# One planner for every expert block of a mixture-of-experts layer

## The chip, the cores and the metric

One NeuronCore of a Trainium2 chip runs the whole program. The metric is device time in microseconds (us) of one execution; a median of runs is given, and one further execution was recorded by the hardware profiler. The engines are TensorE (PE, matmuls), VectorE (DVE), ScalarE (ACT), GpSimd (POOL) and SyncE (SP, which here only issues DMAs). Each engine works through its own instructions strictly in order; semaphores tie the engines together.

## The reference

There are 16 sequences of 256 tokens with 256 features, 4096 tokens in all. `x` goes through an adapter with a layer norm; every token is then given to two of eight experts, and all tokens also go through one shared expert:

```python
y = adapter_layernorm(x, profile_id)               # per sequence
p = softmax(y @ gate_w + gate_b); v, i = top_k(p, 2); v = v / (v.sum() + 1e-9)
mlp(y, w1, b1, w2, b2) = gelu(y @ w1 + b1) @ w2 + b2        # 256 -> 1024 -> 256
out = x + y + mlp_shared(y) + sum_k v_k * mlp_expert[i_k](y)
```

## The kernel before

**Blocks.** Tokens are sorted by expert through DRAM. A *unit* is one block of 256 tokens of one expert (`nt=2`) or of 128 tokens (`nt=1`, a half block). Units 0 to 15 are static: two for each of the eight experts. Units 16 to 36 take what is left: 16 full blocks and five half blocks (`HALF_AT`), whose expert is read from a table at run time. Each number is split into two fp16 parts, so that a product takes three matmuls.

**One unit.** `mm1` (L669) makes eight chunks of the hidden layer, six matmuls each; ACT applies the gelu to each chunk (L676) from one of four PSUM banks into one of two `h` buffers; after four chunks DVE or ACT writes the high half of `hh` (L686 or L684) and DVE the low half (L690); `mm2` (L705) makes the output in eight pieces of six matmuls; DVE takes it out of PSUM (`take`, L1249), and POOL scatters the rows to the DRAM tensor `yrow` with an indirect DMA (`scatter_y`, L1255). A half block has matmuls of 128 columns in `mm1` and four pieces in `mm2`.

**What feeds a unit.** `block_T` (L1242, L1246) brings the transposed tokens and their row numbers, `block_weights` (L1606, L1608) two weight pieces of 1 MB and a small tail, into one of three weight buffers, for a full block only if the expert changed. Both are issued by SP.

**The early sums.** Six of the sixteen sequences (`EARLY = 6`) get their weighted expert sums while the late blocks still run. Such a sum needs a load of the sequence's rows of `yrow` (`y_load`, L1631, 512 KB, on SP) and four DVE operations (`combine`, L1648), after which SP stores the sequence. A load reads `yrow`, so it waits for the scatters that stand ahead of it in the program. In the same stretch SP loads each sequence of `x` again (`x_again`, L1664), and POOL adds it and a bias (`add_x`, L1669 and L1670).

**Order.** Two mechanisms set the order of instructions. Class `Plan` is a list scheduler: each operation has an engine (or a choice of two), a planned duration, things it must wait for (`deps`, after their planned end; `after`, after their planned start), buffers it takes from pools, and a wish time `v`. `schedule` always takes the operation that can start first; `v` decides between equals. In the kernel before, the plan covers everything up to the first half of unit 13. From there to the end of the shared block 13 a loop written by hand follows (L1681 to L1712). It sets the order of SP and POOL; the order on PE, DVE and ACT follows the framework's own scheduling of that recording. In it `unit_steps` alternates chunk c of a unit's `mm1` with piece c of the unit before in `mm2`; at step 7 of unit s the loop stores sequence s-23, sums sequence s-22 and loads sequence s-21:

```python
if n == 7:
    b = s - EARLY_AT - 2
    if 0 <= b < EARLY: store(b)
    b = s - EARLY_AT - 1
    if b in early: combine(b, early.pop(b), lean=True)
    b = s - EARLY_AT
    if 0 <= b < EARLY: early[b] = y_load(early_buf[b % 2], 2 * b, 2)
```

**The end.** All engines then meet at a branch (L1714, L1715) that would do rare extra blocks. After it a second, small plan does the rest of the shared blocks 13 to 15 and the sums of sequences 6 to 15 (L1759 to L1793). There a sequence in `POOLED` (the even ones) has its second addend scaled by ACT (L1773) and added by POOL (L1788); the others take two more DVE operations (L1780).

Of the kernel before, what the change touches and what calls it, by code (L numbers as in the profile page):

```python
# [19 lines left out]
P = 128  # L20
# [4 lines left out]
E = 8  # L25
# [12 lines left out]
EARLY_AT = TOP_AT + 3  # L38
# [13 lines left out]
NPLAN = 14  # L52
# [3 lines left out]
POOLED = tuple(range(0, NB, 2))  # L56
# [95 lines left out]
VE2 = 8.9  # L152


@with_exitstack
def adapter_moe_kernel(
# [559 lines left out]
    def plan_unit(k, v, xin, w, tail, evac, x_deps, w_deps, t_deps, only1=False, xrel=(), free_hi=True):  # L716

        w1 = views(w)[0]
        g1, ge, quads = [], [], []
        for c in range(NC):  # L720
            a = ("u", k, c)
            vc = v + 1.29 * c
            g1.append(
                plan.op(
                    "PE", 0.645, lambda c=c, a=a: mm1(pa_of(a), xin(), w1, c, BLK), vc,
                    [*x_deps, w_deps[0]] + g1[-1:], acq=[("pa", a)], lat=0.25,
                    rel=xrel if c == NC - 1 else (),
# [6 lines left out]
                    "ACT", 0.5,  # L734
                    lambda c=c, a=a, hb=hb: gelu(
                        h32b[plan.slot["h32", hb]], pa_of(a), tail, c, BLK
# [4 lines left out]
            if c % 4 == 3:  # L741
                def hi(act, q=q, hb=hb):
                    split_hi(hhb[plan.slot["hh", k]], h32b[plan.slot["h32", hb]], tail, q, BLK, act)

                def lo(q=q, hb=hb):
                    split_lo(hhb[plan.slot["hh", k]], h32b[plan.slot["h32", hb]], tail, q, BLK)

                h = plan.op(
                    ("DVE", "ACT") if free_hi else "ACT", (0.87, 1.1) if free_hi else 1.1,
# [5 lines left out]
                    plan.op("DVE", 1.28, lo, vc + 2.0, [h], rel=[("h32", hb)], lat=0.05)  # L755
# [3 lines left out]
        plan_g2(k, v + 10.3, w, evac, [quads[0], quads[1]], w_deps[1])  # L759
        return g1  # L760

    def plan_g2(k, v, w, evac, quads, w_dep):
        w2 = views(w)[1]
        g2 = []
        for c in range(2 * 4):
            q, t = place(c, 2)
            r = (f"py{t}", k)
            g2.append(
                plan.op(
                    "PE", 0.645,  # L770
                    lambda q=q, t=t: mm2(py_of(t, k), hhb[plan.slot["hh", k]], w2, q, t),
                    v + 1.29 * c + 0.65, [quads[0 if q < 2 else 1], w_dep] + g2[-1:],
                    acq=[r] if q == 0 else (), rel=[("hh", k)] if c == 7 else (), lat=0.25,
                )
            )
            if q == 3:
                evac(t, g2[-1], v + 1.29 * c + 1.5, (r,))

# [345 lines left out]
    def table(last):  # L1124
# [104 lines left out]
        plan.op("DVE", 1.0, meta, 300.0, [got])  # L1229
        plan.op("DVE", 0.1, lambda: V.memset(spot, 0.0), 0.0, [got, o], add=["pa", "py0", "py1"])  # L1230
        return got, pads
# [21 lines left out]
    def scatter_y(ysb, idt, t):  # L1253
# [9 lines left out]
        apart("ysc", ins)  # L1263

# [59 lines left out]
    def shared(b, only1=False):  # L1324
        def evac(t, mm, v, rel):
# [9 lines left out]
            ("s", b), U0 + b * PU, lambda: xlnT[:, b], halves(wsh), tsh, evac,  # L1335
            [tc_done[b]], pE.done, [pE.tail1], free_hi=False,
        )

    for b in range(NSH):
        shared(b)  # L1340
    got, pads = table([s for sc in scats for s in sc])
# [20 lines left out]
    def static_unit(s):  # L1362
        u = units[s]
        e = s // NSTAT
        vu = U0 + (NSH + s) * PU
        BT[s] = plan.op(
            "SP", 5.2,
            lambda: block_T(u, xgb[plan.slot["xg", s]], idb[plan.slot["id", s]]),
            vu - 22.0, [got, *pads, null_row, *[o for sc in scats for o in sc]],
            acq=[("xg", s), ("id", s)], land=2 * P * 1024,  # L1370
        )

        def evac(t, mm, v, rel):
            ty = plan.op(
                "DVE", 0.45,
                lambda: take(ysbb[plan.slot["ysb", (s, t)]], py_of(t, ("e", s)), u["tail"]),
                v, [mm, prep[e].tail, prep[e].bias], acq=[("ysb", (s, t))], rel=rel,
            )

            def sc():  # L1380
                scatter_y(ysbb[plan.slot["ysb", (s, t)]], idb[plan.slot["id", s]], t)

            plan.op(
                "POOL", 1.36, sc, v + 0.5, [ty],
                rel=[("ysb", (s, t))] + ([("id", s)] if t == 1 else []), land=P * 1024,
# [5 lines left out]
            [BT[s]], prep[e].done, [prep[e].tail], only1=s == NPLAN - 1,  # L1391
            xrel=[("xg", s)],
        )
        g1_last[s] = g1[-1]
# [465 lines left out]
```

## Time and profile before

| what | value |
|---|---|
| median of 3 runs | 651.94 us (650.79 to 653.05) |
| the profiled execution | 656.57 us |
| its span on the core, first to last instruction | 654.8 us |
| PE, busy share of the span | 93% |
| DVE | 63% |
| ACT | 60% |
| POOL | 37% |
| mean granted TensorE clock | 0.959 |
| DMA traffic | 134.71 MB, mean 206 GB/s |

The profile shows one execution. Its page gives busy time by engine, busy tenths in 40 slices of the span (16.4 us each) with the granted TensorE clock, and groups of instructions; further answers of the trace give waits, windows of time and the instructions in order of time.

### The profile page before, as it was taken

What the parts mean: (1) busy time and instruction counts of PE and PEld (TensorE: products, weight loads), DVE (VectorE), ACT (ScalarE), POOL (GpSimd) and SP (SyncE); (2) the same over time, 40 slices, a digit from 0 to 9 for tenths busy, and PEclk for the clock granted to TensorE, in tenths of its full rate; (3) what the DMA queues carried; (4) which work ended last, traced back from release to release, by engine and by line L of the source; (5) the groups of instructions that cost most, each with busy time, mean ns of one, the idle gap of its engine ahead of it and who ended that gap; (6) DMA issues with size and microseconds to landing.
All of it is one profiled execution on the core that took longest, in us unless ns stands there. A gap on an engine that the chain in (4) does not pass through costs nothing. (4 is left out here: it accounts for less than half of the span.)

```text
span 654.8 us, 15253 instructions
## 1 busy us (share of the span) xinstructions
PE 610.2 (93%) x5542; PEld 525.9 (80%) x5542; DVE 414.2 (63%) x992; ACT 390.7 (60%) x609; POOL 241.7 (37%) x367
## 2 busy tenths in 40 slices
PE   4699999999999999999999999999678899999895
PEld 3368887888988888888888888987556789989684
DVE  5678889899863635676658544454347654556377
ACT  1378576796776868879889544444232344444462
POOL 1003466285386013232222122333336455645222
PEclk8579999999999999999999999999797899999899
DMA  7775559847322394978995598288787579990093
GB/s 261 256 273 165 174 189 320 292 188 244 135 95 88 88 276 130 261 247 217 246 301 170 111 363 241 54 202 215 240 262 238 135 228 341 168 282 27 23 376 106
DMA packets 95784, 134.71 MB, mean 206 GB/s; under 512 B 53691, under 2 KB 73173, under 8 KB 87766
## 3 DMA queue, kind: packets, MB, share of 16 engines
q1 hardware_dynamic: 88130, 113.09, 59.0%
q0 software_dynamic: 6768, 18.43, 8.3%
q10 hardware_dynamic: 804, 2.16, 1.0%
q8 instruction: 45, 0.74, 0.4%
q14 instruction: 37, 0.30, 0.2%
HBM read 96.46 MB, written 44.42 MB: 215 GB/s over the span
## 5 line engine op out<-in xcount | busy, mean ns | idle before, releaser
L705 PEld LDWEIGHTS <-hh 128*128 128x128 f16 x2424 | 235.2, 99 | 51.1 <-DVE hh L686 11.9
L705 PE MATMUL bank<-wst,hh 128*128 128x256 f16 x1536 | 213.7, 277 | 14.2 <-DVE hh L686 9.4
L676 ACT ACTIVATE h<-bank,tst 128x256 f32<-128x256 f32 x256 | 139.5, 562 | 129.4 <-PE bank L669 109.2
L669 PE MATMUL bank<-late,wst 128*128 128x256 f16 x1536 | 205.0, 274 | 0.7 <-ACT h L676 0.7
L1255 POOL DMA_INDIRECT yrow<-late,idt x69 | 88.7, 1286 | 265.3 <-DVE late L1249 224.5
L669 PEld LDWEIGHTS <-wst 128*128 128x128 f16 x1536 | 151.0, 98 | 18.8 <-issue 0.9
L669 PE MATMUL bank<-xlnT,wsh 128*128 128x256 f16 x768 | 106.0, 277 | 3.2 <-ACTq L1715 3.2
L705 PE MATMUL bank<-wsh,hh 128*128 128x256 f16 x768 | 102.6, 274 | 3.1 <-DVE hh L690 3.1
L676 ACT ACTIVATE h<-bank,tsh 128x256 f32<-128x256 f32 x128 | 70.1, 561 | 58.0 <-PE bank L669 55.3
L690 DVE SCALAR_TENSOR_TENSOR hh<-h,tst,hh 128x1024 f16<-128x1024 f32 x64 | 85.7, 1339 | 17.1 <-ACT hh L684 16.2
L669 PEld LDWEIGHTS <-wsh 128*128 128x128 f16 x768 | 75.3, 100 | 15.0 <-issue 3.7
L1099 POOL DMA_INDIRECT xslot<-late,sli x64 | 71.6, 1118 | 38.5 <-issue 22.5
L686 DVE TENSOR_SCALAR hh<-h,tst 128x1024 f16<-128x1024 f32 x45 | 39.8, 885 | 72.1 <-ACT h L676 72.0
L1249 DVE SCALAR_TENSOR_TENSOR late<-bank,tst 128x256 f32<-128x256 f32 x64 | 30.6, 478 | 35.6 <-PE bank L705 34.6
L690 DVE SCALAR_TENSOR_TENSOR hh<-h,tsh,hh 128x1024 f16<-128x1024 f32 x32 | 41.0, 1281 | 17.4 <-ACT hh L684 17.2
L676 ACT ACTIVATE h<-bank,late 128x128 f32<-128x128 f32 x40 | 18.3, 458 | 32.7 <-PE bank L669 23.4
L684 ACT ACTIVATE hh<-h,tsh 128x1024 f16<-128x1024 f32 x31 | 35.6, 1147 | 0.8
L1088 POOL IOTA late<- 128x32 int32 x32 | 4.8, 162 | 75.1 <-PE bank L965 39.5
L1648 DVE SCALAR_TENSOR_TENSOR base<-xlnT,wts,base 128x256 f32<-128x256 f32 x24 | 10.4, 479 | 34.2 <-DMA xlnT<-yrow 34.1
L624 DVE SCALAR_TENSOR_TENSOR wst<-wf,prep,wst 128x1024 f16<-128x1024 f32 x20 | 25.3, 1276 | 0.1
L1670 POOL TENSOR_TENSOR base<-base,sb_b 128x512 f32<-128x512 f32 x16 | 23.4, 1462 | 1.3
L830 PE MATMUL bank<-xlnT,wst 128*128 128x256 f32 x64 | 19.7, 436 | 4.1 <-DMA wst<-in_adp_dram 4.1
(233 smaller groups left out, 599.5 us busy)
## 6 DMA issues: line engine op xcount, KB each, us to landing
wst<-scr SPq DMA_DIRECT2D x32, 1024.0 KB
scr<-wst SPq DMA_DIRECT2D x16, 1024.0 KB
wf<-scr SPq DMA_DIRECT2D x10, 1024.0 KB
wf<-in_ew_dram SPq DMA_DIRECT2D x5, 1028.0 KB
wf<-in_ew_dram SPq DMA_DIRECT2D x5, 1024.0 KB
wst<-in_adp_dram SPq DMA_DIRECT2D x16, 256.5 KB
xlnT<-in_xT_dram SPq DMA_DIRECT2D x16, 256.0 KB
base<-in_x_dram SPq DMA_DIRECT2D x16, 256.0 KB
```

The source lines that it names most:

```text
L624: V.scalar_tensor_tensor(self.w[:, a + 2048 : b + 2048], self.wf[h][:, f], sc[:, 2 * h : 2 * h + 1], self.w[:, a:b], ALU.mult, ALU.subtract,)
L669: mm = PE.matmul(pa[:, 0:n_tok], w1[:, wl, c, k, :], xin[:, xl, k, 0:n_tok], start=i == 0, stop=i == len(seq) - 1,)
L676: ACT.activation(h32[:, c % 4, 0:n_tok], pa[:, 0:n_tok], AF.Gelu_apprx_tanh, bias=tail[:, c : c + 1], scale=tail[:, 8:9],)
L684: ACT.activation(hi, h4, AF.Copy, scale=tail[:, 9:10])
L686: V.tensor_scalar(hi, h4, tail[:, 9:10], None, ALU.mult)
L690: V.scalar_tensor_tensor(hh[:, 1, c, 0:n_tok], h32[:, :, 0:n_tok], tail[:, 9:10], hh[:, 0, c, 0:n_tok], ALU.mult, ALU.subtract,)
L705: PE.matmul(py, hh[:, hl, k, t * P : (t + 1) * P], w2[:, wl, k, :], start=q == 0 and i == 0, stop=q == 3 and i == len(seq) - 1,)
L830: PE.matmul(pt_of(("z", b))[:, 0:S], wa()[:, k * P : (k + 1) * P], xf32(b)[:, k, :], start=k == 0, stop=k == KC - 1,)
L1099: ins = POOL.indirect_dma_start(out=xslot[:, :], out_offset=bass.IndirectOffsetOnAxis(ap=sli[:, c, j : j + 1], axis=0), in_=payb[plan.slot ...
L1249: V.scalar_tensor_tensor(ysb, py, tail[:, 10:11], tail[:, 11 : 11 + D], ALU.mult, ALU.add)
L1255: ins = POOL.indirect_dma_start(out=yrow[:, :], out_offset=bass.IndirectOffsetOnAxis(ap=idt[:, t, :].bitcast(I32), axis=0), in_=ysb, in_of ...
L1670: POOL.tensor_tensor(bb, bb, sb2_b.unsqueeze(1).broadcast_to([P, 2, D]), ALU.add)
```

## The change

`plan_unit` and `plan_g2` learn half blocks (`nt=1`) and a looser rule for expert blocks and late shared blocks: a chunk follows the one before it by its planned start, no longer by its planned end. `static_unit` becomes `expert_unit`, which plans all 37 units, with their weight loads (`W`), and with wish times 10.32 us apart, where static ones had 16.4. Reloads of `x`, the additions on POOL, the loads of `yrow`, each single addition of an early sum and the stores become operations of the same plan. The reloads of `x` are issued from ACT's queue instead of SP's. The load of sequence b is planned for unit b+22, its sum for unit b+23, the store for b+24. The hand-written loop with its helpers goes. In the last plan all sequences but 14 and 15 use ACT and POOL for the second addend.

```diff
     def plan_unit(..., nt=2, behind=None):
+        n, step = nt * P, 0.645 * nt
+        full = nt == 2
+        loose = k[0] == "e" or k[1] >= NSH
...
-                    "PE", 0.645, lambda c=c, a=a: mm1(pa_of(a), xin(), w1, c, BLK), vc,
-                    [*x_deps, w_deps[0]] + g1[-1:], acq=[("pa", a)], lat=0.25,
+                    "PE", 0.645 if full else 0.5, lambda c=c, a=a: mm1(pa_of(a), xin(), w1, c, n), vc,
+                    [*x_deps, w_deps[0]] + ([] if loose else g1[-1:]), acq=[("pa", a)], lat=0.25,
+                    rel=xrel if c == NC - 1 else (), after=g1[-1:] if c else [behind],
...
-    def static_unit(s):
+    def expert_unit(s, vu):
         u = units[s]
-        vu = U0 + (NSH + s) * PU
+        nt = u["nt"]
+        last = None if s == 0 else BT[s - 1]
         BT[s] = plan.op(
-            "SP", 5.2,
+            "SP", 2.6 * nt,
             lambda: block_T(u, xgb[plan.slot["xg", s]], idb[plan.slot["id", s]]),
-            vu - 22.0, [got, *pads, null_row, *[o for sc in scats for o in sc]],
+            vu - TV, [got, *pads, null_row, *[o for sc in scats for o in sc]],
+            after=[last] if s >= NS else [], acq=[("xg", s), ("id", s)], land=nt * P * 1024,
+        )
...
+            W[s] = plan.op(
+                "SP", 2.4, lambda: block_weights(u), vu - WV, deps, acq=acq, land=P * (6500 if nt == 2 else 13000)
+            )
...
-            prep[e] = Prep(e, U0 + (NSH + NSTAT * (e - 1)) * PU - 8.0, after=after, split_after=split)
+            prep[e] = Prep(e, v_of(NSTAT * (e - 1)) - VP, after=after, split_after=split)
...
+    for b in range(NB):
+        s = TOP_AT + 1 + b
+        o = plan.op(
+            "ACT", 0.45,
+            lambda b=b, xr=xr: ACT.dma_start(
+                xr, x[b * S : (b + 1) * S, :].rearrange("(t p) d -> p t d", p=P)
+            ), vu_of[s], wf_free, after=[g1_of[s][2]], acq=[("xr", ("xr", b))], land=P * 2048,
+        )
+        x_op = plan.op(
+            "POOL", 2.6, add_x, vu_of[s] + 12, [o], rel=[("xr", ("xr", b))],
+            after=[g1_of[s + 1][2]] if s + 1 < NU else [],
+        )
+        if b < EARLY:
+            s += 3
+            o = plan.op(
+                "SP", 0.45, lambda b=b, yl=yl: y_load(yl, 2 * b, 2), vu_of[s],
+                [*wf_free, sc_last[NS - 1]], after=[g1_of[s][3]], acq=[("ey", ("ey", b))],
+                land=P * 4096,
+            )
+            for i in range(4):
+                o = plan.op(
+                    "DVE", 0.45, lambda b=b, yl=yl, i=i: sum_one(b, yl, i // 2, i % 2, wts),
+                    vu_of[s + 1] + 6, [o, wts_op], after=[g1_of[s + 1][4]] if i == 0 else [],
+                    rel=[("ey", ("ey", b))] if i == 3 else (),
+                )
+            plan.op("SP", 0.45, lambda b=b: store(b), vu_of[s + 2], [o, x_op], after=[g1_of[s + 2][3]])
+
+    shared(NSH, v_end, only1=True)
...
-    with tc.manual_schedule(engines={ET.SP, ET.Pool}):
-        xr = None
-        early = {}
-        for s in range(NPLAN, NU):
-            u = units[s]
-            for n, _ in enumerate(unit_steps(block_unit(u))):
-                if n == 6 and s + 2 < NU:
-                    next_T(units[s + 2])
-                if n == 7:
...
-            if NS <= s + 2 < NU and units[s + 2]["nt"] == 2:
-                block_weights(units[s + 2])
-            if xr is not None:
-                add_x(s - TOP_AT - 2, xr)
-            if TOP_AT < s <= TOP_AT + NB:
-                xr = x_again(s - TOP_AT - 1)
...
-                    if c == 1 and bb in POOLED:
+                    if c == 1 and bb < NB - 2:
                         done.append(plan.op(
                             "ACT", 0.42,
...
-                            "DVE", 0.45,
+                            "DVE", 0.48,
```

## The prediction

> **What bounds the kernel now.** I read the page's slices first. TensorE is nearly always busy, so what counts is where it is not.
>
> ```profile
> PE   4699999999999999999999999999678899999895
> PEclk8579999999999999999999999999797899999899
> ```
>
> Apart from start and end, one hole stands in slices 29 to 32 (458 to 524 us), where the granted clock drops as well. Windows of 20 us sharpen it (columns: window, length, then busy us and instruction count of PE, PE weight loads, DVE, ACT, POOL, then clock, DMA share, GB/s):
>
> ```profile
> 400.00:420.00 20.00, 20.00 (x195) 18.04 (x193) 9.72 (x12) 8.82 (x17) 5.02 (x7) 1.00 0.52 154
> 440.00:460.00 20.00, 18.57 (x182) 16.32 (x180) 8.67 (x11) 8.04 (x15) 6.34 (x6) 1.00 0.81 194
> 460.00:480.00 20.00, 13.13 (x102) 10.37 (x100) 9.37 (x19) 4.28 (x9) 7.50 (x9) 0.83 0.83 256
> 480.00:500.00 20.00, 14.48 (x110) 11.43 (x108) 10.14 (x12) 5.91 (x11) 9.24 (x8) 0.83 0.70 207
> 500.00:520.00 20.00, 17.90 (x179) 15.76 (x177) 13.39 (x20) 7.83 (x15) 9.12 (x10) 0.99 0.81 225
> ```
>
> PE idles 1.43 + 6.87 + 5.52 + 2.10 = 15.9 us in the last four. No engine is full there, so this is a chain of waits. The wait lists, PE's, DVE's and SP's in turn, name its links (total, times, longest):
>
> ```profile
> PE bank L705 <- DVE hh L686: 10.7, 5, 4.5
> PE bank L705 <- DVE hh L690: 8.6, 9, 2.7
> ```
>
> ```profile
> DVE base L1648 <- DMA xlnT<-yrow: 34.1, 6, 7.4
> ```
>
> ```profile
> SPq L1631 <- DMA yrow<-late,idt: 55.2, 7, 29.3
> ```
>
> PE waits for the split of `hh` on DVE, DVE stands six times before an early sum (L1648) until its load of `yrow` has landed, and that load waits on SP for a scatter (the 29.3 is a seventh, at the end). The timeline shows one turn:
>
> ```profile
> 450.58 1.77 POOL L1255 DMA_INDIRECT yrow<-late,idt  x1 [0.34 <-DVE late L1249]
> ...
> 457.63 0.39 SPq L1631 DMA_DIRECT2D xlnT<-yrow  x1
> ...
> 461.33 1.27 DVE L1648 SCALAR_TENSOR_TENSOR base<-xlnT,wts,base 128x256 f32<-128x256 f32 x3 [6.58 <-DMA xlnT<-yrow]
> 463.31 0.74 DVE L686 TENSOR_SCALAR hh<-h,tst 128x1024 f16<-128x1024 f32 x1
> 464.11 0.39 PE L705 MATMUL bank<-wst,hh 128*128 128x256 f16 x2 [3.72 <-DVE hh L686]
> ```
>
> From the scatter's issue to the load's is 7.05 us, from there to the sum 3.70: 10.75 us. DVE is idle for 6.58 of them with the finished gelu behind the sum in its queue. The takes wait behind it too, hence the next scatter is late, hence the next load: the six stalls (6.04, 6.58, 7.39, 7.44, 2.35, 4.30 us) feed each other. Afterwards the clock costs more. Two groups of six matmuls in a cold stretch and two after it, by their starts:
>
> ```profile
> 495.18 1.49 PE L669 MATMUL bank<-late,wst 128*128 128x256 f16 x6
> 496.46 1.49 PE L705 MATMUL bank<-wst,hh 128*128 128x256 f16 x6
> ...
> 499.67 0.82 PE L669 MATMUL bank<-late,wst 128*128 128x256 f16 x6
> 500.32 0.82 PE L705 MATMUL bank<-wst,hh 128*128 128x256 f16 x6
> ```
>
> 1.28 us a group against 0.65. Over the three cold stretches (465.7 to 472.0, 494.35 to 499.0, 519.2 to 523.5) the groups take 2.9 + 2.3 + 1.7 = 6.9 us more than at 0.655. The hole costs 15.9 + 6.9 = **22.8 us**.
>
> **Part 1, the early sums.** In the built order I count the matmuls between the three instructions (0.109 us for 256 columns, half for 128). Before, scatter to sum is 5.9, 6.1, 5.5, 5.2, 5.9 and 6.9 us of matmuls against the 10.75 needed. In the changed kernel it is 13.7, 14.1, 9.3, 19.7, 15.7 and 14.1, since the sum moves one unit behind the load. Five are clear by 3 us or more; the third is short by 1.4 us. Before, a DVE stall of 2.35 us cost PE nothing and one of 4.30 cost 2.1 plus the cold 1.7, so I take 0.5 for it (0 to 2). SP still stands up to 7 us before such a load, with token and weight loads behind it; in the built order these lead their first matmul by 12.8 us or more at nearly every late unit (9.5 at two; least before, 9.0), so that is hidden; without this cover each late us is one of PE's. Gain 22.8, loss 0.5.
>
> **Part 2, blocks 14 to 36 in the plan.** Matmuls, gelus, splits, takes and scatters keep number and shape. From 525 to 600 us PE shows no idle in the old alternation, so there is nothing to win. The plan places `mm2` as soon as its inputs are ready by its own durations. Most are near the trace (gelu 0.58 with latency against 0.56, split 0.87 and 1.28 against 0.753 and 1.283); two are not. Six matmuls of 128 columns are planned at 0.5 us and start 0.33 apart, so PE arrives up to 8 x 0.17 = 1.4 us early at what it needs, in five half blocks: 0 to 7 us. And the plan does not know that POOL's 32 additions slow DVE: a low split of 1.28 us took 2.55 beside one. About 2 us of slack stand against that after the last chunk (four alternations of 1.31 = 5.2 us less the chain 0.56 + 0.75 + 1.28 and waits). I take 1.0, nearer to the old order's nothing.
>
> **Part 3, reloads of `x` on ACT.** Sixteen issues of 0.39 us leave SP (6.2 us, hidden there: SP was not on PE's chain but for part 1) and come to ACT. ACT usually idles 0.74 us before each gelu, which hides an issue. New is that ACT waits in order: for POOL's addition two sequences back (7.3 to 16.7 us of matmuls ahead in the built order), and, through shared DMA semaphores, twice for a 1 MB weight piece issued 5.2 and 5.6 us ahead. Behind a waiting ACT stand gelus, behind them PE, covered by four banks, some 5 us in alternation. With pieces landing in 4 to 8 us (1 and 2 MB at 256 GB/s) ACT stands up to 3 us in two places: 0 to 2 us of PE, I take 0.5.
>
> **Part 4, static blocks.** Wish times closer together bring preparations and loads forward relative to the shared blocks. PE idles 1.2 us from 180 to 440, so the bounds are -1.2 and, with ACT 19 of 20 us busy around 350, some +3; I take +0.5. The branch keeps its 3.2 us of PE idle.
>
> **Part 5, the tail.** From 631.5 to 651.5 us the chain that ended last is DVE. DVE loses six operations, 6 x 0.48 = 2.9 us; ACT gains six copies of 0.50, four of them ahead of the last split in its queue; POOL gains three additions. The answer for the additions' line shows how a DVE operation fares beside POOL (min/median/max ns):
>
> ```profile
> L1780 DVE SCALAR_TENSOR_TENSOR base<-wst,wts,base x18: 471/479/1552, 636.8 to 650.3; 128x256 f32<-128x256 f32 x18
> L1788 POOL TENSOR_TENSOR base<-base,wst x3: 1262/1387/1397, 638.1 to 648.2; 128x512 f32<-128x512 f32 x3
> ```
>
> The 30 operations took 18.1 us instead of 30 x 0.48 = 14.4, 0.74 for each of five additions, so three more cost 2.2 and the tail would gain 0.7. The Trainium skill speaks against that (*SBUF — State Buffer*, "SBUF: two separate sides"): VectorE and GpSimd hold a shared port pair for a whole instruction and the loser blocks fully. At 1.3 us each, three more cost 3.9 and the tail loses 1.0. The longest operation, 1.55 us, lies nearer to the page; with the copies ahead of the split I take +0.5 (-2.9 to +2.5).
>
> **Sum.** -22.8 + 0.5 + 1.0 + 0.5 + 0.5 + 0.5 = -19.8. The profiled span 654.8 becomes 635.0, its execution 656.57 becomes 636.8. That execution lies 4.6 above the median of the runs, so the forecast for the median is 651.94 - 19.8 = **632.1 us**.
>
> **Rivals.**
> *Half a gain.* The loads come later than their place says, since POOL carries scatters and additions in one queue and a scatter must itself wait for an earlier load, so three sums still stall. For: the third sum has no slack. Against: the others have 3 to 9 us. Keeping 10 of the 22.8 gives 642.
> *DVE becomes the bound.* With sums in place DVE does 6.9 us a unit (two high splits 1.5, two low 2.6, two takes 1.0, four sums 1.9) and up to 2.5 beside POOL, 9.4 of PE's 10.5. Against: only six units. If the plan's exact placing costs 0.5 us in each of the 23 late units, 11.5 in all, the result is 643.
> *The stall only moves* to another late link (a weight load, a take), PE keeps its hole: 652. Against: leads as above.
> *Slower.* The reloads hold ACT, one mechanism: POOL's addition or a weight piece late, ACT stopped in the gelus. From about 5 us of hold on, PE pays one for one; with 19.8 gained elsewhere the sixteen reloads decide above 1.2 us each, about 6.4 us of hold every time. At 8 us each it is 632 + 16 x 3 less the 0.5 already in the sum, about 680. Against: POOL was 37% busy, and POOL's additions lead by 7.3 us or more.
>
> **How the numbers follow.** Forecast 0.69, half a gain 0.11, DVE or the exact order 0.10, only moved 0.05, slower 0.05. The forecast's own range is 627 (tail and static blocks at their best) to 638. The range for 8 in 10 is 626 to 643: it takes in the two middle rivals and leaves out the last two and their neighbours. Two kernels under 0.3% (2 us) apart can't be told apart here. Faster by more: 0.69 + 0.11 + 0.10 = 0.90, less 0.01 for a middle rival that goes further; the 0.05 of a stall that only moved splits into 0.03 same and 0.02 slower, so same is 0.04 and slower 0.07.
>
> **What would show it.** Right: no PE wait for L686's successor over 1 us between 440 and 505, clock 1.00 in those windows, the sums' wait for `yrow` down from 34.1 us to under 5, last expert matmul about 20 us earlier. Part 3 wrong: ACT waits on DMA or POOL before a gelu of over 4 us. Part 2 wrong: many PE waits of 0.3 to 1 us on `hh`. Part 5: the stretch from branch to end, 36 us now, over 38. The forecast falls if the third sum starts the old convoy again, or if a weight piece comes late behind a waiting load.

## The result: a smaller gain than forecast

The changed kernel takes 644.58 us (median of four runs, 641.56 to 645.63); the kernel before took 652.50 beside it (650.79 to 654.18). The ratio is 0.987, with a 95% interval of 0.983 to 0.992. Forecast were 632.1 us, in a range of 626 to 643: the sign is right, the size is not. In a later session (e5 below) the ratio was 0.981 (0.973 to 0.989). Every ratio here leaves out runs more than 1.5% above the fastest of the same kernel, which matters only for e3 and e4 below, where four of six runs and ten of 22 fall out.

The profiled executions differ by more than the medians: their spans are 654.8 and 642.1 us. The prediction had found that the profiled execution of before lies 4.6 us above its median; that of the changed kernel (643.85 us) lies 0.7 below its own. So of the 12.7 us between the spans some 5 belong to these two executions.

**A ledger of TensorE's loss.** I count each trace back from its end in matmul work (0.1092 us for 256 columns, half for 128) and set the time against it. What is over is idle time or a low clock. "Late" is the stretch from the point where 170 us of this work are left to the branch (143.8 us of work), "tail" is the rest, from the branch to the end.

```
                      before    changed
start of late stretch  446.6      443.6
loss in it              25.0       13.5
branch reached         615.5      600.9
loss in the tail        13.1       15.0
```

So -3.0 ahead of the stretch, -11.5 in it, +1.9 in the tail: -12.6 us, the difference of the spans but for rounding. Of the 3.0, 1.3 belong to Part 4 (below). The other 1.7 lie still earlier, where three traces of the old plan (this one, e17 and e18) differ among themselves by 2.9. The page's slices of the changed kernel show the same:

```profile
PE   5599999999999999999999999999988998999795
PEclk7779999999999999999999999999999999999798
```

The two slices at 8 and the 8 further on are the old hole, flatter; its clock stays up. The windows of 20 us (columns as in the prediction):

```profile
440.00:460.00 20.00, 20.00 (x209) 18.20 (x207) 10.31 (x15) 12.12 (x22) 4.05 (x6) 1.00 1.06 264
460.00:480.00 20.00, 17.93 (x161) 15.29 (x159) 7.00 (x12) 8.31 (x15) 8.50 (x11) 1.00 0.75 215
480.00:500.00 20.00, 16.47 (x172) 14.54 (x170) 13.95 (x19) 10.06 (x20) 11.51 (x12) 1.00 0.81 249
500.00:520.00 20.00, 19.45 (x179) 17.18 (x178) 13.73 (x18) 9.91 (x17) 12.32 (x14) 1.00 0.65 164
520.00:540.00 20.00, 16.82 (x175) 14.89 (x173) 6.64 (x8) 9.43 (x18) 10.89 (x13) 1.00 1.00 352
```

From 460 to 540 us PE idles 2.1 + 3.5 + 0.6 + 3.2 = 9.4 us, where it idled 14.5 before; the clock, 0.83 in two of these windows before, is 1.00. The lists of waits of PE and of DVE (whole trace: total, times, longest) say on what; of the first line, the longest wait (3.2) lies in the tail and 3.9 us lie ahead of the branch:

```profile
PE bank L704 <- DVE hh L689: 7.3, 8, 3.2
PE bank L668 <- ACT h L675: 6.3, 4, 2.5
```

```profile
DVE base L1534 <- DMA xlnT<-yrow: 9.5, 5, 3.6
```

The sums (L1534, before L1648) wait 9.5 us for `yrow` instead of 34.1, and still five times. PE's second line is all but new (0.7 us, once, before): PE waits for gelus. ACT's list between 440 and 604 us shows why these are late:

```profile
ACT h L675 <- DMA late<-xslot: 8.1, 2, 7.1
ACT h L675 <- DMA out_dram<-base: 6.2, 1, 6.2
ACT h L675 <- POOL base L1562: 5.3, 2, 3.0
```

No gelu needs the store `out_dram<-base`. The reload of `x` in front of it in ACT's queue does: it shares a DMA semaphore with that store, and the other rows are a shared semaphore and POOL's addition.

At first sight the reloads are the culprit. The next view says otherwise. The timeline of the changed kernel, lines of SP, DVE and POOL in order of time:

```profile
446.73 1.03 SPq L1289 DMA_DIRECT2D wst<-scr  x2
447.85 0.39 SPq L1523 DMA_DIRECT2D xlnT<-yrow  x1
...
456.24 1.92 DVE L1534 SCALAR_TENSOR_TENSOR base<-xlnT,wts,base 128x256 f32<-128x256 f32 x4 [1.15 <-DMA xlnT<-yrow]
...
457.25 1.06 SPq L1289 DMA_DIRECT2D wst<-scr  x2
...
459.57 1.00 POOL L1267 DMA_INDIRECT yrow<-late,idt  x1 [12.98 <-DVE hh L689]
...
460.88 0.97 POOL L1267 DMA_INDIRECT yrow<-late,idt  x1 [0.19 <-issue]
...
468.09 0.39 SPq L1523 DMA_DIRECT2D xlnT<-yrow  x1
...
471.86 1.40 DVE L1534 SCALAR_TENSOR_TENSOR base<-xlnT,wts,base 128x256 f32<-128x256 f32 x3 [3.21 <-DMA xlnT<-yrow]
```

From one load of `yrow` (447.85) to the next (468.09) are 20.2 us. The first is issued 1.1 us behind 2 MB of weights in the same queue: by the trace's packets, the weights' 256 of 8 KB run from 447.71 to 454.31 and the load's 256 of 2 KB from 453.32 to 455.65. POOL has nothing to do for 13 us, although the take for its next scatter was done at 449.2: in the program this scatter waits first of all for the load to have landed, since it writes the tensor that the load reads, and that wait ends at 456.17. So scatter, load and next scatter form a loop, each waiting for the one before; a round of it, from load to load, is called a turn below. The scatter after it, issued at 460.88 beside the next 2 MB of weights, has its last packet at 467.36, and the next load waits for that. The sum, at 456.24, stood 1.15 us. It is a reader at the side of this loop, not a link in it.

How far this loop lags I measure as each scatter's start, less the start of the matmul beside which it stands in the built order (start : us late):

```
before   435:0.5 449:7.3 451:5.8 465:10.5 467:9.8 477:7.6 479:6.4 493:10.1 502:2.7 503:1.2 515:5.3 517:4.9 522:0.9
changed  442:0.3 460:10.4 461:9.2 473:12.3 480:14.2 481:15.3 493:12.2 494:12.3 502:11.6 503:10.5 512:7.7 516:8.5 518:9.9 523:3.2 524:1.0
```

In both kernels the lag comes with the first load and goes some 15 us after the sixth. In the changed kernel it is the larger one. The six loads themselves are 3.4, 13.2, 13.0, 10.3, 11.2 and 7.7 us behind their places: the first turn, with weights beside both its load and its scatter, puts the loop 9.8 us back, and four more turns (7.4, 12.2, 8.9 and 9.9 us) win back 5.5.

### The profile page after: what moved, and what is told of

Same layout as the page of the kernel before. It is cut to its first block, busy times and chain, and to the rows that moved or that the text cites. A ratio compares the mean times of both kernels' runs of the same rounds, so it can differ in the third digit from the quotient of the medians.

```text
span 642.1 us, 15142 instructions
## 1 busy us (share of the span) xinstructions
PE 605.6 (94%) x5542; PEld 522.8 (81%) x5542; DVE 405.8 (63%) x969; ACT 404.3 (63%) x632; POOL 234.2 (36%) x370
## 5 line engine op out<-in xcount | busy, mean ns | idle before, releaser
L675 ACT ACTIVATE h<-bank,tst 128x256 f32<-128x256 f32 x256 | 136.0, 560 | 127.8 <-PE bank L668 86.8
L704 PE MATMUL bank<-wst,hh 128*128 128x256 f16 x1536 | 205.8, 273 | 3.3 <-DVE hh L689 3.3
L668 PE MATMUL bank<-late,wst 128*128 128x256 f16 x1536 | 200.4, 273 | 5.0 <-ACT h L675 4.3
L1267 POOL DMA_INDIRECT yrow<-late,idt x69 | 77.6, 1125 | 256.7 <-DVE late L1261 202.6
L704 PE MATMUL bank<-wsh,hh 128*128 128x256 f16 x768 | 104.7, 277 | 3.4 <-DVE hh L689 3.4
L675 ACT ACTIVATE h<-bank,tsh 128x256 f32<-128x256 f32 x128 | 70.1, 560 | 58.7 <-PE bank L668 55.1
L689 DVE SCALAR_TENSOR_TENSOR hh<-h,tst,hh 128x1024 f16<-128x1024 f32 x64 | 89.4, 1396 | 27.5 <-ACT hh L683 26.0
L668 PEld LDWEIGHTS <-wsh 128*128 128x128 f16 x768 | 75.5, 100 | 15.5 <-issue 3.8
L685 DVE TENSOR_SCALAR hh<-h,tst 128x1024 f16<-128x1024 f32 x27 | 21.3, 787 | 46.3 <-ACT h L675 46.3
L689 DVE SCALAR_TENSOR_TENSOR hh<-h,tsh,hh 128x1024 f16<-128x1024 f32 x32 | 42.0, 1311 | 13.4 <-ACT hh L683 13.1
L683 ACT ACTIVATE hh<-h,tst 128x1024 f16<-128x1024 f32 x37 | 42.5, 1148 | 1.1
L683 ACT ACTIVATE hh<-h,tsh 128x1024 f16<-128x1024 f32 x29 | 33.3, 1147 | 0.8
L1100 POOL IOTA late<- 128x32 int32 x32 | 4.8, 161 | 73.4 <-PE bank L977 37.8
L1562 POOL TENSOR_TENSOR base<-base,xlnT 128x512 f32<-128x512 f32 x16 | 20.6, 1285 | 8.2 <-DMA xlnT<-in_x_dram 8.0
```

Of the source, the lines that this page charges most:

```text
L668: mm = PE.matmul(pa[:, 0:n_tok], w1[:, wl, c, k, :], xin[:, xl, k, 0:n_tok], start=i == 0, stop=i == len(seq) - 1,)
L675: ACT.activation(h32[:, c % 4, 0:n_tok], pa[:, 0:n_tok], AF.Gelu_apprx_tanh, bias=tail[:, c : c + 1], scale=tail[:, 8:9],)
L683: ACT.activation(hi, h4, AF.Copy, scale=tail[:, 9:10])
L685: V.tensor_scalar(hi, h4, tail[:, 9:10], None, ALU.mult)
L689: V.scalar_tensor_tensor(hh[:, 1, c, 0:n_tok], h32[:, :, 0:n_tok], tail[:, 9:10], hh[:, 0, c, 0:n_tok], ALU.mult, ALU.subtract,)
L704: PE.matmul(py, hh[:, hl, k, t * P : (t + 1) * P], w2[:, wl, k, :], start=q == 0 and i == 0, stop=q == 3 and i == len(seq) - 1,)
```

## The experiments

Theories: the reloads of `x` hold ACT (1), or the rest of the old convoy costs the time (2; in e1's expectation theory 2 is still the plan's exact order). The second was later split into DVE's sums (A) and the loop of load and scatter alone (B). All results are in one table; medians are of all runs, and "late" and "tail" are TensorE's losses in the one profiled execution, in us. Two traces of the changed kernel itself differ by 1.3 us in the late stretch, so a difference of that size between two rows shows nothing. The expectations quote 24.8 and 13.2 for the late stretches of the two kernels, from a cut that ended 7 us of work ahead of the branch; the table cuts at the branch.

```
                         median  before  ratio (95%)             late  tail
changed, first time      644.58  652.50  0.987 (0.983 to 0.992)  13.5  15.0
e1  reloads on SP        664.29  674.51  0.987 (0.983 to 0.990)  12.1  13.5
e2  old tail             664.48  674.51  0.987 (0.982 to 0.992)  13.0  13.1
e3  both                 663.10  674.51  0.975 (0.968 to 0.983)  13.6  11.7
e4  old, sums later      674.17  674.51  0.995 (0.992 to 0.998)  22.5  13.4
e5  changed, again       640.85  653.92  0.981 (0.973 to 0.989)  12.2  13.9
e6  reloads on POOL      640.88  653.92  0.983 (0.977 to 0.990)  10.9  14.0
e7  no reloads, adds     638.18  653.92  0.979 (0.972 to 0.985)   8.2  15.1
e8  no loads, sums       632.88  653.92  0.971 (0.964 to 0.977)   2.6  15.5
e9  loads, no sums       643.54  654.72  0.983 (0.978 to 0.987)  13.6  14.2
e10 pairs                637.77  654.72  0.975 (0.970 to 0.981)   6.8  15.0
e11 pairs, POOL          636.99  654.72  0.974 (0.969 to 0.979)   3.9  14.3
e12 pairs, POOL, tail    634.35  654.72  0.970 (0.965 to 0.974)   4.0  13.6
e13 loads first          664.59  675.34  0.987 (0.978 to 0.997)  15.4  12.3
e14 loads first, POOL    662.39  675.34  0.983 (0.975 to 0.991)  11.2  15.1
e15 loop alone           658.78  675.34  0.977 (0.969 to 0.984)   7.1  13.9
e16 first, pairs, etc.   662.76  675.34  0.980 (0.972 to 0.988)  10.4  15.5
e17 old, no loads, sums  632.69  653.47  0.967 (0.962 to 0.973)   0.4  14.9
e18 old, pairs           642.74  653.47  0.983 (0.978 to 0.988)  13.2  13.4
```

Runs e1 to e4 and e13 to e16 were on two other chips, where every kernel, the one before included, takes some 20 us more, all of it ahead of the late stretch; so ratios and late losses are compared, not times. e7, e8, e9, e15 and e17 leave out work that the result needs; they show only what a part costs.

**e1, reloads back on SP.**

```diff
-            "ACT", 0.45,
-            lambda b=b, xr=xr: ACT.dma_start(
+            "SP", 0.45,
+            lambda b=b, xr=xr: SP.dma_start(
```

> The changed kernel with one thing undone: the sixteen reloads of x are issued by SP again, in the plan, in place of ACT. Theory 1 (ACT stands in front of its gelus because a reload in its queue waits for a DMA or for POOL's addition): ACT's waits for DMA and POOL before a gelu, 25 us between 440 and 604 us in the changed kernel's trace, are gone, PE's waits for gelus (6.3 us) go and most of those for the low split (3.9 us) with them; time 635 to 639 us, 0.975 to 0.980 of the kernel before. Theory 2 (the plan's exact order, or DVE beside POOL's additions, costs the missing gain): time as the changed kernel, 642 to 646 us, 0.985 to 0.991. Theory 3 (SP needed the relief: its weight loads now come late behind waiting reloads): 650 us or more.

Ratio 0.987, theory 2's number. ACT's waits for DMA and POOL are gone as theory 1 said. But PE still waits 7.6 us for other things (10.9 in the changed kernel), its clock falls to 0.86 in the window from 500 to 520 us, and the late stretch loses 12.1 us. The two largest rows of its waits between 460 and 625 us:

```profile
PE bank L668 <- DMA wst<-scr: 3.5, 2, 1.9
PE bank L704 <- DVE hh L689: 2.8, 2, 2.2
```

With the reloads in SP's queue it is the weights behind them that come late.

**e2 and e3, the old share of the final sums**, alone and with e1.

```diff
-                    if c == 1 and bb < NB - 2:
+                    if c == 1 and bb % 2 == 0:
...
-            if bb < NB - 2:
+            if bb % 2 == 0:
```

> The changed kernel with the final sums shared out as before (ACT copies and POOL additions for every second sequence, not for all but the last two). Theory 1 (the new share costs the tail 1.7 us, 37.84 us from PE's restart behind the branch to the end against 36.15): 642 to 643.5 us, stretch 36 to 36.5 us. Theory 2 (the tail's difference is the clock's, cold for longer behind the branch): stretch stays at 37 to 38 us, time 644 to 645 us.

> Both of the two edits before this one: reloads of x by SP, final sums shared out as before. If both theories 1 hold the gains add up: 633 to 637 us. If neither does: 642 to 646 us.

e2 changes the time by nothing that can be told, and its tail loses 13.1 us against 15.0 and 13.9 of the two traces of the changed kernel. e3's ratio looks better, but it rests on two of six runs, one of them (652.04) 9 us under the other five; the median of all six is 0.983 of the kernel before's. Its late stretch is no better (13.6), its tail is the shortest of all. Over all traces the tail loses 12.3 to 15.5 us with the new share (twelve traces, mean 14.3) and 11.7 to 15.5 with the old (eight, mean 13.6). A difference of 0.7 us within such a spread isn't shown.

**e4, the old kernel with the sums one unit later.**

```diff
-                    b = s - EARLY_AT - 2
+                    b = s - EARLY_AT - 3
...
-                    b = s - EARLY_AT - 1
+                    b = s - EARLY_AT - 2
```

> The kernel before, with nothing but the early sums (and the stores behind them) moved one unit later; blocks 14 to 36 stay outside the plan, reloads of x stay on SP. Theory 1 (the hole between 440 and 525 us is the sums' place alone): the sums' wait for yrow falls from 34.1 us to under 10, the hole's 22.8 us go but for 2 to 5: 632 to 636 us, 0.970 to 0.976. Theory 2 (the hole has other causes too, which only the plan's order takes away): 641 to 648 us. Theory 3 (the sums wait as before in the new place, since the load is what is late): 650 to 653 us.

No theory was tested. In the built order only the stores moved; the scheduler, which orders DVE there, put all 24 sums at the very places where they had stood. They waited 5.7, 6.8, 6.6, 7.5, 2.4 and 4.2 us, as before. The medians of all runs are alike (674.17 and 674.51); the 0.995 comes from the runs that this ratio leaves out, ten of 22 here and one of 27 of the kernel before. So the edit changed nothing that can be told.

**e5 to e8: the changed kernel, and what each suspect costs when it is left out.** e6 puts `POOL` in the place of `ACT` in the lines of e1 (planned at 1.0 us, not 0.45). The other two keep all operations in the plan, so that the order stays, and empty them:

```diff
# e7: neither reload nor addition of x
-            lambda b=b, xr=xr: ACT.dma_start(
-                xr, x[b * S : (b + 1) * S, :].rearrange("(t p) d -> p t d", p=P)
-            ), vu_of[s], ...
+            lambda: None, vu_of[s], ...
         def add_x(b=b, xr=xr):
             bb = base[:, 2 * b : 2 * b + 2, :]
+            return
# e8: neither load of yrow nor early sum
-                "SP", 0.45, lambda b=b, yl=yl: y_load(yl, 2 * b, 2), vu_of[s],
+                "SP", 0.45, lambda: None, vu_of[s],
-                    "DVE", 0.45, lambda b=b, yl=yl, i=i: sum_one(b, yl, i // 2, i % 2, wts),
+                    "DVE", 0.45, lambda: None,
```

> The changed kernel unaltered, so that the next three stand beside it on one chip. All theories: 0.983 to 0.992 of the kernel before; between the last 170 us of PE's work and the branch it loses 11 to 15 us to idle time and a low clock (13.2 in its first trace; the kernel before 24.8).

> The changed kernel with one edit: the reloads of x are issued by POOL, whose queue holds the additions that free their buffers, so that neither ACT nor SP waits for them. In the built order twelve of the sixteen wait at most for a scatter or load over 20 us of matmuls old. Theory 1 (whichever queue carries the reloads pays for their waits: ACT's gelus, or SP's weight loads): the late stretch loses 13.2 us less 6 to 9, ratio 0.970 to 0.978. Theory 2 (the rest of the old convoy of scatter, load and early sum is what costs, the reloads are innocent): 11 to 15 us lost as before, ratio 0.983 to 0.992. Theory 3 (issuing costs POOL about 1 us each, scatters get later): ratio above 0.992.

> The changed kernel in the same order with the sixteen reloads of x and POOL's additions of x and of the bias left out (the output lacks both): what they cost altogether. Theory 1: ACT's waits for DMA and POOL are gone and the late stretch loses under 6 us of 13.2; ratio 0.970 to 0.977. Theory 2: it still loses 9 us or more; ratio 0.980 to 0.990.

> The changed kernel in the same order with the loads of yrow and the 24 early sums left out (the first six sequences lack the experts' part), reloads and additions of x kept on ACT: what is left of the sums' convoy. Theory 1: ACT is still held by the reloads, the late stretch loses 7 us or more of 13.2; ratio 0.977 to 0.987. Theory 2: it loses under 4 us; ratio 0.968 to 0.975.

Late losses 12.2, 10.9, 8.2 and 2.6. e6 and e8 are as theory 2 has them, e7 lies between the two. The reloads and additions together are worth 4.0 us; loads and sums are worth 9.6. The reloads' queue makes 1.3, which is no more than two traces of one kernel differ by. e8 still has every reload on ACT, and PE's waits from 440 to 605 us, the branch's 3.4 included, are nearly gone:

```profile
PE bank L668 <- ACTq L1631: 3.4, 1, 3.4
PE bank L668 <- ACT h L675: 1.2, 1, 1.2
```

Scatters are then at most 4.0 us late. So a reload on ACT costs almost nothing if the scatters are on time. Without the reloads, DVE's sums stand longer than in the changed kernel (16.3 us for 9.5), but what stops PE is mostly late weights (e7, waits of PE and DVE):

```profile
PE bank L668 <- DMA wst<-scr: 3.3, 2, 2.6
...
DVE base L1534 <- DMA xlnT<-yrow: 16.3, 6, 3.7
```

**e9 to e12: sums or loop, and fewer turns of the loop.** e9 makes only the second edit of e8. "Pairs" loads two sequences at once, at every second unit, into two buffers of double size (blocks 4 to 7 and 9 to 12 of `xlnT`):

```diff
+    pair_buf = [y_view(flat[:, o * 1024 : (o + 4) * 1024], 4) for o in (4, 9)]
+    ld = {}
...
-            s += 3
-            yl = early_buf[b % 2]
-            o = plan.op(
-                "SP", 0.45, lambda b=b, yl=yl: y_load(yl, 2 * b, 2), vu_of[s],
+            s += 4 - b % 2
+            g = b // 2
+            yl = pair_buf[g % 2]
+            if b % 2 == 0:
+                ld[g] = plan.op(
+                    "SP", 0.45, lambda b=b, yl=yl: y_load(yl, 2 * b, 4), vu_of[s], ...
+            else:
+                s += 1
+            o = ld[g]
+            yl = yl[:, 2 * (b % 2) : 2 * (b % 2) + 2]
```

> The changed kernel in the same order with the six loads of yrow kept and the 24 early sums left out (the first six sequences lack the experts' part). It splits the loss that went with loads and sums together (11.9 us to 2.4 in the late stretch). Theory A (DVE hands it on: it stands in its queue before a sum, splits and takes behind it): gone here too, 2 to 4 us lost, 632 to 635 us on a chip where the kernel before takes 652 to 654 (ratio 0.969 to 0.974). Theory B (the loop of load and scatter is enough: a scatter waits for the load before it, the next load for that scatter, takes wait for buffers that late scatters hold): 7 us or more lost, ratio 0.977 to 0.987.

> The changed kernel with three loads of yrow of two sequences each, at every second unit, in place of six of one sequence at every unit; the sums stay one unit behind the load or two. Reloads of x stay on ACT. Theory A+B (a turn of scatter, load and next scatter takes 12 us or more, a unit of PE only 10.5, so the turns fall behind one another): with 21 us a turn there is time, late stretch loses 4 to 7 us of 11.9 to 13.2, ratio 0.970 to 0.979. Rival (each load is late by itself, behind weights in flight, however far apart): 9 us or more, ratio 0.981 to 0.990.

> The edit before this one, and the reloads of x issued by POOL. If the loop is loosened, ACT's holds are the next cost (no reload and no addition won 4 us with the loop in place; their issue by POOL 1): late stretch 1 to 4 us, ratio 0.967 to 0.974. If they are hidden once the loop is loosened: as the run before this, within 1 us.

> Both edits before this one and the final sums shared out as before. Tail (from the branch to the end) over all traces so far: 13.7 to 15.8 us above PE's work with the new share, 11.9 to 13.6 with the old. So 1 to 2 us less than the run before this; ratio 0.964 to 0.972. If the tail's difference is chance: no less.

e9 decides for B: with not one early sum, 13.6 us are lost as in the changed kernel, and the scatters lag up to 14.6 us. PE's loss now comes almost wholly through ACT (waits of PE and ACT, 440 to 605 us):

```profile
PE bank L668 <- ACT h L675: 9.2, 5, 2.8
...
ACT h L675 <- DMA late<-xslot: 7.7, 2, 6.5
ACT h L675 <- DMA idt<-xslot: 7.3, 1, 7.3
```

Pairs take the loss to 6.8, with POOL's queue to 3.9, as forecast. The price of a turn in the expectation, 12 us or more, was too simple, though: after the first one three of four took less than 10, and what pairs give is time to make good a slow one, and half as many of them. The same bytes in half as many loads lose half as much, so it is not the loads' traffic that costs. The reloads' queue makes 2.9 us here, more than in e6. e12 has the best ratio of all kernels that leave nothing out: 0.970 of the kernel before, where the changed kernel, in other sessions, had 0.987 and 0.981 (its interval just touches the second one's). It also overlaps that of e11, so the old tail's share in it isn't shown. Its slices and its waits of PE (440 to 605 us):

```profile
PE   4599999999999999999999999999999899999794
...
PEclk8579999999999999999999999999999999999899
```

```profile
PE bank L668 <- ACTq L1639: 3.4, 1, 3.4
PE bank L704 <- DVE hh L689: 3.1, 3, 2.3
```

**e13 to e16: the place in SP's queue, and the loop alone.** The loads are planned earlier, so that five of six stand ahead of the weights that they stood behind:

```diff
-                "SP", 0.45, lambda b=b, yl=yl: y_load(yl, 2 * b, 2), vu_of[s],
-                [*wf_free, sc_last[NS - 1]], after=[g1_of[s][3]], acq=[("ey", ("ey", b))],
+                "SP", 0.45, lambda b=b, yl=yl: y_load(yl, 2 * b, 2), vu_of[s] - 16,
+                [*wf_free, sc_last[NS - 1]], after=[g1_of[s][0]], acq=[("ey", ("ey", b))],
```

e14 adds POOL's queue, e15 is e9 and e7 together, e16 is e12 with this edit.

> The changed kernel with the six loads of yrow placed 1 to 4 us earlier in SP's queue, so that five of them stand ahead of the weight pieces that they stood behind; sums, scatters and reloads keep their place. Theory Q (the load's packets run behind 2 MB of weights in SP's queue, and with that the loop falls behind at its first turn): the first load lands in 3 to 4 us, not 8.3, the scatters of the next unit are under 4 us late, not 9, the late stretch loses 4 to 8 us of 11.9 to 13.2; ratio 0.971 to 0.980. Theory N (six turns are too many, wherever they stand): 10 us or more lost, ratio 0.981 to 0.990.

> The edit before this one and the reloads of x issued by POOL. If ACT's holds come only from a late loop: within 1.5 us of the run before this. If ACT's waits on shared DMA semaphores cost by themselves: 2 to 4 us less.

> The changed kernel in the same order with the six loads of yrow kept, and sums, reloads of x and additions of x left out (the output lacks them). If a late loop stops TensorE by itself (takes wait for buffers that late scatters hold): 6 us or more lost in the late stretch. If only through DVE's sums or ACT's reloads: 1 to 3 us, as without loads.

> Three loads of two sequences, ahead of the weights, reloads of x by POOL, final sums shared out as before. If queue and number of turns both count: late stretch 1 to 3 us (3.9 with pairs, POOL and the old tail), ratio 0.964 to 0.970. If pairs have taken all of it: as that run, 0.9695.

e13 shows the queue's part in the first turn and no gain. The first load is issued at 465.4, its packets end at 468.5, and the scatters behind it are 3.7 and 3.2 us late in place of 10.4 and 9.2. But the third load, the one that still stands behind weights, is issued at 483.6 and its packets end at 491.6; from there on the scatters are 7.7 to 12.5 us late and ACT stands before a reload (waits of PE and ACT, 460 to 625 us):

```profile
PE bank L668 <- ACT h L675: 9.3, 4, 4.8
...
ACT h L675 <- DMA xlnT<-yrow: 8.7, 2, 7.0
...
ACT h L675 <- POOL base L1562: 6.4, 1, 6.4
```

So theory N holds for the loss as a whole: one slow turn anywhere was enough, since those behind it made good too little. e14 is 4.2 us better in the late stretch, so the share of the reloads' queue is 1.3 to 4.2 us in three comparisons of single traces; in none of the three are the times themselves clear of each other. e15 answers the other question: the lag stops PE by itself too, 7.1 us, and the path is SP, where loads that wait for scatters have put the weights 12 us behind their place:

```profile
PE bank L668 <- DMA wst<-scr: 4.7, 1, 4.7
```

e16 came out worse than e12 (10.4 against 4.0), though its scatters are at most 5.9 us late; that both edits add up is refuted. PE waits 6.6 us there for low splits, 4.5 of it once. In its trace that split stands in DVE's queue behind five sums, which take 5.83 us where 5 x 0.479 is 2.4, while POOL makes four additions (512.76 to 519.70); in the window from 520 to 540 us the clock is then 0.83:

```profile
515.07 5.83 DVE L1534 SCALAR_TENSOR_TENSOR base<-xlnT,wts,base 128x256 f32<-128x256 f32 x5
...
521.62 1.03 PE L704 MATMUL bank<-wf,hh 128*128 128x256 f16 x4 [4.48 <-DVE hh L689]
```

That is the mechanism of the rival "DVE becomes the bound", in one place. No run takes it out.

**e17 and e18: the same two questions in the old kernel.** e17 takes `combine` and `y_load` out of the loop over units, e18 loads pairs there, and has loads, sums and stores one unit later:

```diff
-                    b = s - EARLY_AT - 2
+                    b = s - EARLY_AT - 3
...
-                    b = s - EARLY_AT - 1
+                    b = s - EARLY_AT - 2
...
-                    b = s - EARLY_AT
-                    if 0 <= b < EARLY:
-                        early[b] = y_load(early_buf[b % 2], 2 * b, 2)
+                    b = s - EARLY_AT - 1
+                    if b in (0, 2, 4):
+                        yl = y_load(pair_buf[b // 2 % 2], 2 * b, 4)
+                        early[b], early[b + 1] = yl[:, 0:2], yl[:, 2:4]
```

> The kernel before with the early loads of yrow and the early sums left out (the first six sequences lack the experts' part), all else as it was. If the loop is the whole of the hole: the late stretch loses 1 to 3 us of 24.8, as the changed kernel does without them (2.4); ratio 0.963 to 0.972. If the old order has a part in it: 5 us or more.

> The kernel before with three loads of two sequences in place of six of one, the sums one or two units behind as written (the scheduler puts all of a load's sums about 4.5 us of matmuls behind it in VectorE's queue). If turns are what counts: half of the hole or less is left, 8 to 13 us of 24.8, ratio 0.980 to 0.988. If the sums' place behind the load counts as much: 14 us or more, ratio 0.985 to 0.995.

e17: the old order loses 0.4 us in the late stretch when the early loads and sums are gone; the only wait of PE left there is the branch's:

```profile
PE bank L669 <- ACTq L1709: 3.4, 1, 3.4
```

So the early loads and sums made the whole hole, the loop and the sums that DVE stands before; no run of the old kernel parts these two, as e9 does in the changed one. Without them the plan's order (2.6 us lost in e8) is no better than the old one. e18: half as many turns, half the loss, 25.0 to 13.2. That is as much as the whole change won in this stretch.

## Why the prediction went wrong

**The step that failed is Part 1.** It counted the matmuls from a scatter to the sum in the built order, compared them with the 10.75 us needed, and booked 22.8 won against 0.5 lost. Two things in this were wrong. The scatter was taken to run at its place; in the changed kernel it runs 9 to 15 us behind it from the second turn on (the first, 0.3 us late, has its 13.8 us and its sum stands 1.15 us). And the need was taken as a delay, once per sum, where it is the time of a turn: scatter, load, and by the write-after-read wait the next scatter. The five turns took 58.7 us, where the loads' places are 47.7 us of matmul work apart (54.5 in the trace, with PE's own waits), and began 3.4 late. The need of 10.75 was also one of six: from scatter to sum it took 6.5 to 12.4 us in the kernel before and 6.5 to 14.7 in the changed one, most in the first turn, whose load runs behind weights. Moving the sum lengthens its own allowance and leaves the turn as it was. The term measured 9.6 us (e5 less e8) where 0.5 was booked, range 0 to 2.

**The sum, too, carried something over.** It took 19.8 us off the median, but had read them from one execution that lay 4.6 us above that median. Of the 12.5 us between forecast and median, 7.1 stand in the traces (a span of 642.1 for 635.0): 9.3 too little won in the late stretch, 3.5 more than booked ahead of it, 1.4 more lost in the tail. The other 5.4 are the places of the two profiled executions among their runs.

The prediction came close. It wrote that the stalls "feed each other", and its rival "half a gain" names the scatter that "must itself wait for an earlier load", at 642 us and 0.11. That was the right one, but I argued it down with the same distances. Its count of stalled sums (three) was wrong: five stood, two of them over 3 us, and with no sum at all the loss is as large (e9).

**Part 2** (+1.0): the late stretch of e8, with reloads on ACT included, loses 2.6 us against 0.4 in the old order (e17). Together with Part 3 (+0.5) 1.5 was booked, 2.2 found: close, as far as two single traces can tell.

**Part 3** (+0.5): its mechanism is in ACT's list, holds of up to 7.1 us and thus over the 4 us that were named as the sign of its failure. By itself the term is small; behind a late loop three comparisons make it 1.3 to 4.2 us. Its cover was the distance to POOL's addition, 7.3 to 16.7 us of matmuls, and POOL's lag of 9 to 15 us ate this cover (5.3 us of ACT's list). The longest hold is another: that reload shares a semaphore with a transpose that SP issued behind 4 MB of weights, whose packets end at 530.81.

```profile
521.49 1.27 SPq L1254 DMA_TRANSPOSE late<-xslot  x1
...
532.25 1.93 ACT L675 ACTIVATE h<-bank,tst 128x256 f32<-128x256 f32 x4 [7.14 <-DMA late<-xslot]
```

Without loads and sums (e8) no hold by a DMA is over 2.8 us. So it failed with Part 1.

**Part 4** (+0.5, bounds -1.2 and +3): the 230 us of work ahead of the late stretch lose 1.2 us instead of 2.5, in every one of the sixteen traces that have the new plan. That is -1.3, at the lower bound; 1.0 of it is PE's idle time between 340 and 360 us, which is gone.

**Part 5** (+0.5, -2.9 to +2.5): +1.9 in the first pair of traces, 0.7 in the means, not resolved. The stretch from branch to end was 37.8 us, under the 38 named. The two prices for an addition can be told apart, though. In the changed kernel's tail DVE's 24 sums take 9.6 + 5.9 = 15.5 us where 24 x 0.479 is 11.5, two high splits take 2.3 for 1.5 and four low ones 6.0 for 5.1: 5.7 us for eight additions, 0.71 each. The row's 0.74 holds. By the Trainium skill (*SBUF — State Buffer*, "SBUF: two separate sides") a VectorE operation with two SBUF inputs, as these sums have, and a GpSimd operation that reads SBUF share a port pair: whichever starts first has it for its whole instruction, and the other blocks. Priced at 1.3 us of DVE for every addition, as in the prediction, that would give 10.4. But POOL's own additions stretch here too (1.26 to 2.18 us), so it is this price that fails; the runs don't speak against the rule. DVE did shed some 0.9 us (18.1 to 15.5 in the sums, 1.7 more in the splits; 0.7 were forecast by the row). PE did not end sooner: it waited 3.23 us for the last low split (2.70 before) and its last 22 matmuls then took 3.94 us instead of 2.58. The timelines, before and changed:

```profile
647.30 2.58 PE L705 MATMUL bank<-wsh,hh 128*128 128x256 f16 x22 [2.70 <-DVE hh L690]
...
634.37 3.94 PE L704 MATMUL bank<-wsh,hh 128*128 128x256 f16 x22 [3.23 <-DVE hh L689]
```

**The other signs.** Clock 1.00 from 440 to 500: came. No wait of PE for the high split (now L685) over 1 us between 440 and 505: came, there is none; for the low split (L689) there are three, up to 1.2 us. Sums' waits under 5 us: failed, 9.5. Last expert matmul some 20 us earlier: failed, 14.6.

## What to carry to other kernels

Before moving the reader of a late transfer, follow the writer's own waits round: where the next write must wait for this read, write and read make a turn that has to fit the period of the work with time to spare, and slack after the reader did not help here. Fewer, larger turns did. And count a distance from where an instruction ran in the trace, not from where it stands in the program: a queue's lag ate the cover of everything that waited on that queue.

## What the runs showed of the hardware

A load behind large transfers in its own queue started only as they ended: issued at 447.85, its packets began at 453.32, 1.0 us before the weights' last one ended, and with the weights behind it (e13) 1.0 us after the issue. The Trainium skill has it so for each engine of a queue (*DMA: Bandwidth & Descriptors*, "Queues, rings and completion order": descriptors are consumed in ring order), and these packets agree.

An engine's queue was held by a DMA that has nothing to do with its work: a reload on ACT waited 6.2 us until a store had landed whose semaphore it shares.

One gap stays unexplained. POOL's wait for the load ended at 456.17, its scatter began at 459.57, and no wait fills these 3.4 us; in two later scatters the same step takes 0.8 us. A 16 KB transfer of instructions runs from 457.80 to 458.86, which may be it.
